# New places for the small loads at the start, and for the first and last pairs of graphs, in a two-layer graph attention kernel

## The chip, the cores and the metric

The kernel runs on one core of a Trainium2 chip. Such a core has a matrix engine (TensorE, PE in the profile), a vector engine (VectorE, DVE), an engine for functions of one argument (ScalarE, ACT), a general one (GpSimd, POOL), one that mostly issues transfers (SyncE, SP), and 16 DMA engines that move data between the main memory and the on-chip memory. Each engine works through a list of its own, in order. The metric is the time of one execution in microseconds (us); lower is better. Three executions gave a median of 2377.61 us (2377.54 to 2379.04).

## The reference

128 graphs, each of 128 nodes with 512 features, all in fp32, go through two layers. All graphs share one 128 x 128 adjacency matrix `adj`.

```python
# layer 0: attention with 8 heads of 64, masked by adj
q, k, v = (x @ Wq + bq), (x @ Wk + bk), (x @ Wv + bv)      # split into 8 heads
scores = q k^T / sqrt(64) + (1 - adj) * -1e9
out = softmax(scores) v                                     # heads joined again
x = layernorm(x + out @ Wo + bo)
# layer 1: graph attention with one head
h = x @ W
e = leaky_relu((h a1)[:, None] + (h a2)[None, :], 0.2) * adj
h' = softmax(e) h
x = layernorm(x + elu(h' + beta * h))
```

## The kernel before

**Pairs.** Two graphs are worked on at a time: 64 pairs, NG = 64, graphs 2g and 2g+1. Pair g is planned STEP = 36.678 us after pair g-1, and several pairs overlap.

**A pair's work.** The x of a pair is fetched twice: as four blocks of 512-byte rows (`load_blocks`, L81, one buffer xblk), which VectorE transposes into xT (`turn_x`, L240), and as whole graphs (`load_x`, L91), to which GpSimd adds the output bias for the residual sum (`residual`, L435). Each of the five large products (q, k, v, the output product w, and h of layer 1) is made from a two-by-two splitting of its matrices, with seven block products in place of eight: GpSimd makes sums of blocks of the input (`block_sum`, L260, tiles tx, tw, th), sums of the weights (s_q, s_k, s_v, s_w, s_h; `weight_sum`, L223 to L229) are made once at the start, TensorE makes the block products (`product`, L301 and L307, into pq, pk, pv, pw, ph and, for the products that serve both halves, eq, ev, ew, eh), and ACT (`take_part`, L349 and L355) and VectorE (`add_block`, L365) bring them together in qT, kT, v, w and h.

**Attention.** Scores (L379, psc), mask (L387), row maxima (L395), exponentials (L401) and the normalised weights (L415) follow. These go to main memory (`attn_write`, L422, tile scr) and come back in another order by four reads (`attn_read`, L427, tile ab); VectorE transposes them (`turn_attn`, L444, attnT), and TensorE multiplies by v (`attend`, L454, po). After the output product and the layer norm (L472 to L522, x1), layer 1's logits are built from two row products (L505) and brought across partitions (L536 to L556, pb, or a transfer through s2d), and its attention is applied (`aggregate`, L642, pz, evicted to zT at L649). ELU follows (L653 to L662), then the last norm (`shift` L714 on VectorE, `norm_f` L720 on ACT) and the store (L726 on SP).

**Order.** Nothing is scheduled by a planner at build time. Every step has a written place: `at(place, step, ...)` records it, all steps are sorted by place, and are emitted in that order; each engine's list is the part of it that the engine executes. `rows(g)` lists the steps of a pair with common places, `last_rows(g)` those of the last two pairs, and `other` replaces the places for pairs 0 to 3, NG-4 and NG-3. A place is a planned time, and not a wait: an instruction runs once those ahead of it on its engine are done and its inputs and buffers are there.

**The start.** x of pair 0 (four transfers), the biases and wq are issued first, from SP and ACT. GpSimd builds the identity and issues adj (L151) and, in `load_later` (place 0.583), beta, the two halves of a and the output bias bo, each broadcast to 128 rows (L104). adj is needed for the mask (`make_mask`), beta for a scaled identity (`make_beta`), a for `wa_column` (L180), which multiplies layer 1's weight by a, and bo for the residual. TensorE runs 30 matmuls on the identity (`keep_busy`, L136) and turns the biases (L140) ahead of the first product. wk and wv are issued on SP in `load_k_and_v`, wo and w1 in `load_weight`.

**The end.** The last pair's output product and h product are made in plain form (L336 and L671), for which parts of wo and w1 are loaded again into wq_sb and wk_sb (`load_again`, L124). Its graphs are normed and stored in halves (L682 to L710). The tiles u_124 to u_127 of the last two pairs are written in two buffers (tag `uf`, two buffers), so that u_126 follows u_124 in the same memory.

Of the kernel before, what the change touches and what calls it, by code (L numbers as in the profile page):

```python
# [18 lines left out]
STEP = 36.678  # L19
# [3 lines left out]
def gnn_two_layers(  # L23
# [127 lines left out]
    nc.gpsimd.dma_start(out=adj_sb, in_=adj)  # L151
    later = {}

    def load_later():
        later["beta"] = broadcast(cpool, beta, 1, "beta_b")
        for j in range(2):
            a_j = a1[j * D : (j + 1) * D].rearrange("f o -> (f o)")
            later["a", j] = broadcast(wk2, a_j, D, "uf")
        later["bo"] = broadcast(cpool, bo, D, "bo_b")
# [578 lines left out]
    def at(place, fn, *args):  # L738
        pieces.append((place, len(pieces), fn, args))
# [81 lines left out]
    def last_rows(g):  # L821

        b0, b1 = g * G, g * G + 1
        if g == NG - 2:
# [5 lines left out]
                (-20.065, product, "q", g, 6), (-18.272, product, "q", g, 7),  # L830
                (-17.379, product, "k", g, 7), (-17.337, take_part, "q", g, 6, 1, 0),
                (-16.541, fetch_x, b0), (-16.486, product, "q", g, 2), (-16.091, fetch_x, b1),
                (-15.593, product, "k", g, 1), (-14.7, product, "k", g, 2),
                (-12.947, take_part, "k", g, 1, 0, 0), (-12.481, add_block, "q", g, 2, 0, 0),
                (-12.121, add_block, "k", g, 2, 0, 0), (-10.901, residual, b0),
                (-9.651, residual, b1), (-9.477, product, "q", g, 5),
                (-8.344, take_part, "q", g, 5, 1, 1), (-7.718, product, "k", g, 6),
                (-6.585, take_part, "k", g, 6, 1, 0), (-5.093, product, "k", g, 5),
                (-3.799, take_part, "k", g, 5, 1, 1), (-3.334, product, "q", g, 3),
                (-2.499, add_block, "k", g, 7, 1, 1), (-2.441, product, "k", g, 3),  # L840
                (-2.201, take_part, "q", g, 3, 0, 1), (-2.139, add_block, "q", g, 7, 1, 1),
                (-1.548, product, "k", g, 4), (-1.308, take_part, "k", g, 3, 0, 1),
                (-0.655, product, "q", g, 4), (0.478, add_block, "q", g, 4, 1, 0),
                (1.178, add_block, "k", g, 4, 1, 0), (2.175, scores, b1), (3.322, scores, b0),
                (3.562, mask, b1, 0), (4.182, mask, b1, 1), (4.222, product, "v", g, 1),
                (4.802, mask, b0, 0), (5.285, product, "v", g, 2), (5.422, mask, b0, 1),
                (6.042, row_max, b0), (6.391, take_part, "v", g, 1, 0, 0), (7.182, row_max, b1),
                (7.382, exps, b0, 0), (7.883, product, "v", g, 6), (8.152, exps, b0, 1),
                (8.922, exps, b0, 2), (9.122, add_block, "v", g, 2, 0, 0), (9.692, exps, b0, 3),
                (10.462, exps, b1, 0), (10.481, product, "v", g, 7), (10.682, row_inv, b0),  # L850
                (11.232, exps, b1, 1), (12.002, exps, b1, 2), (12.772, exps, b1, 3),
                (13.793, row_inv, b1), (15.553, normalise, b0, 0), (16.143, normalise, b0, 1),
                (16.733, normalise, b0, 2), (17.323, normalise, b0, 3), (18.133, attn_write, b0),
                (18.917, take_part, "v", g, 6, 1, 0), (21.213, attn_read, b0),
                (21.363, normalise, b1, 0), (21.953, normalise, b1, 1), (23.073, normalise, b1, 2),
                (23.663, normalise, b1, 3), (24.473, attn_write, b1), (25.163, turn_attn, b0, 0),
                (26.143, turn_attn, b0, 1), (27.553, attn_read, b1), (32.523, product, "v", g, 5),
                (33.588, turn_attn, b1, 0), (33.629, take_part, "v", g, 5, 1, 1),
                (34.208, add_block, "v", g, 7, 1, 1), (34.568, turn_attn, b1, 1),
                (35.175, product, "v", g, 4), (36.041, product, "v", g, 3),  # L860
                (36.281, add_block, "v", g, 4, 1, 0), (37.147, take_part, "v", g, 3, 0, 1),
                (38.954, attend, b0), (40.021, attend, b1), (40.261, attend_evict, b0),
                (41.341, attend_evict, b1), (41.954, product, "w", g, 1),
                (42.641, block_sum, "w", g, 1), (42.82, product, "w", g, 2),
                (43.421, block_sum, "w", g, 2), (43.961, take_part, "w", g, 1, 0, 0),
                (44.201, block_sum, "w", g, 4), (44.401, add_block, "w", g, 2, 0, 0),
                (44.981, block_sum, "w", g, 3), (45.418, product, "w", g, 6),
                (46.284, product, "w", g, 7), (46.524, take_part, "w", g, 6, 1, 0),
# [229 lines left out]

    for g in range(NG):
        lay(g)  # L1100
    at(0.583, load_later)
    at(5.685, load_k_and_v)
    at(8.723, weight_sum, "q", 3, nc.vector)
    at(9.443, weight_sum, "q", 1, nc.vector)
# [70 lines left out]
```

## Time and profile before

| what | value |
|---|---|
| median of three executions | 2377.61 us |
| profiled execution | 2378.15 us |
| its span (first to last instruction) | 2376.4 us |
| granted TensorE clock | 0.998 |
| TensorE busy | 2354.4 us, 99% of the span |
| VectorE, ACT, GpSimd busy | 1961.7, 1591.1, 865.5 us |
| moved by DMA | 269.83 MB, 114 GB/s on average |
| wq, wk, wv landed | 10.14, 15.08, 18.15 us |
| blocks of pair 1 landed (last of four) | 23.93 us |
| scores of pair 0 begin | 28.84 us |
| from one pair's scores to the next, in the steady part | 36.50 us |

The span is what the views of the profile cover; 1.75 us of the profiled execution lie outside it. Times in the views count from the span's start. In a timeline a line gives start, duration, engine, kernel line, operation, output and inputs, count, and in brackets how long the engine stood idle before it and what ended that. SPq, POOLq and ACTq are the engines' issues of transfers. The profile names the last thing that a waiting instruction got; where that had long been done, it was another.

### The profile page before, as it was taken

Reading aid. Unit: us, or ns where it says so; the run is one execution under the profiler, and the core shown is the slowest. Engines: PE = TensorE matmul, PEld = TensorE weight load, DVE = VectorE, ACT = ScalarE, POOL = GpSimd, SP = SyncE. Lnnn points to the kernel's source line nnn. Section 1 sums busy time; section 2 is a strip of 40 time slices with the busy share of each in tenths; the row PEclk is TensorE's granted clock in tenths of the full one; section 3 lists DMA queues with packets and bytes.
Section 4 is the critical chain, followed back from the end, with each engine's and each line's share of the span. In section 5 each row is a group of like instructions: output and inputs, shape, how many; then the busy total and the mean of one; then the engine's idle time right before and its main releaser. Section 6 shows DMA issues by size and latency. Waiting matters only on the chain.

```text
span 2376.4 us, 50868 instructions
## 1 busy us (share of the span) xinstructions
PE 2354.4 (99%) x17703; PEld 2177.5 (92%) x17703; DVE 1961.7 (83%) x4390; ACT 1591.1 (67%) x5763; POOL 865.5 (36%) x1044
## 2 busy tenths in 40 slices
PE   8999999999999999999999999999999999999998
PEld 8998999999999999999999999999999999999996
DVE  7788788888888888888888888888888888888887
ACT  4675666766766667667666676676666766766665
POOL 6243333433433333334334333343343333433422
PEclk9999999999999999999999999999999999999999
DMA  6333334334343343343443433424434334344432
GB/s 192 108 100 112 116 101 125 107 105 134 92 120 119 107 118 108 108 128 92 121 122 103 119 108 111 126 92 121 123 103 119 107 112 125 92 120 122 116 115 74
DMA packets 256121, 269.83 MB, mean 114 GB/s; under 512 B 57372, under 2 KB 204840, under 8 KB 255480
## 3 DMA queue, kind: packets, MB, share of 16 engines
q1 hardware_dynamic: 254992, 265.45, 37.8%
q8 instruction: 140, 2.29, 0.4%
q14 instruction: 117, 0.96, 0.1%
q0 software_dynamic: 304, 0.85, 0.1%
q10 hardware_dynamic: 568, 0.27, 0.0%
HBM read 157.62 MB, written 108.85 MB: 112 GB/s over the span
## 4 chain that ended last, share of the span: by engine, by line
PE 96%; DMA 1%; DVE 1%; ACT 1%; issue 0%; SPq 0%; POOLq 0%; POOL 0%; DVEq 0%; ACTq 0%
PE pq L307 12%; PE pk L307 12%; PE pv L301 12%; PE ph L301 11%; PE pw L301 11%; PE eq L307 9%; PE psc L379 5%; PE po L454 5%; PE pz L642 5%; PE eh L301 5%; PE ew L301 4%; PE ev L301 4%; DMA xblk<-in_x_dram 1%; DMA wq_sb<-in_L_gnn_Wq_dram 0%; ACT s L401 0%
## 5 line engine op out<-in xcount | busy, mean ns | idle before, releaser
L435 POOL TENSOR_TENSOR x<-x,bo_b_in 128x512 f32<-128x512 f32 x128 | 163.6, 1279 | 863.3 <-DMA x<-in_x_dram 863.3
L401 ACT ACTIVATE s<-s,nmax 128x128 f32<-128x128 f32 x1024 | 396.9, 396 | 61.4 <-DVE nmax L395 61.3
L415 ACT ACTIVATE sb<-s,rinv 128x128 f32<-128x128 f32 x1024 | 325.3, 392 | 0.0
L355 ACT ACTIVATE kT<-pk,bias_c 128x128 f32<-128x128 f32 x512 | 160.2, 364 | 202.2 <-PE pk L307 143.2
L355 ACT ACTIVATE qT<-pq,bias_c 128x128 f32<-128x128 f32 x512 | 160.6, 368 | 157.6 <-PE pq L307 157.6
L505 DVE SCALAR_TENSOR_TENSOR ya<-w,wa_row 128x512 f32<-128x512 f32 x256 | 223.9, 875 | 4.4
L401 ACT ACTIVATION_READ_ACCUMULATOR s<-s,nmax 128x1 f32 x1024 | 199.2, 195 | 0.0
L466 ACT ACTIVATE oT<-po,bias_c 128x128 f32<-128x128 f32 x512 | 139.5, 382 | 80.5 <-PE po L454 80.5
L352 DVE TENSOR_TENSOR w<-pw,x 128x256 f32<-128x256 f32 x252 | 106.3, 422 | 97.3 <-PE pw L301 90.8
L444 DVE STREAM_TRANSPOSE attnT<-ab 128x512 f32<-128x512 f32 x256 | 172.7, 694 | 6.8 <-DMA ab<-scr 6.6
L387 DVE SCALAR_TENSOR_TENSOR s<-psc,amask 128x512 f32<-128x512 f32 x256 | 168.6, 680 | 0.7 <-PE psc L379 0.7
L395 DVE TENSOR_REDUCE nmax<-s 128x8 f32<-128x1024 f32 x128 | 156.1, 1220 | 4.3
L349 ACT COPY h<-ph 128x256 f32<-128x256 f32 x252 | 93.8, 372 | 94.1 <-PE ph L301 94.0
L349 ACT COPY v<-pv 128x256 f32<-128x256 f32 x256 | 94.6, 369 | 84.4 <-PE pv L301 59.9
L240 DVE STREAM_TRANSPOSE xT<-xblk 128x512 f32<-128x512 f32 x128 | 139.4, 1108 | 7.9 <-DMA xblk<-in_x_dram 7.9
L657 DVE SCALAR_TENSOR_TENSOR u<-h,x 128x512 f32<-128x512 f32 x126 | 87.1, 692 | 63.8 <-ACT h L349 61.6
L260 POOL TENSOR_TENSOR tx<-xT 128x256 f32<-128x256 f32 x128 | 94.7, 741 | 119.8 <-PE psc L379 97.1
L301 PE MATMUL pv<-wv_sb,xT 128*128 128x256 f32 x512 | 137.5, 392 | 0.0
L307 PE MATMUL pq<-xT,wq_sb 128*128 128x128 f32 x1024 | 135.9, 276 | 1.2 <-DMA wq_sb<-in_L_gnn_Wq_dram 1.2
L307 PE MATMUL pk<-xT,wk_sb 128*128 128x128 f32 x1024 | 134.8, 275 | 0.6 <-DMA wk_sb<-in_L_gnn_Wk_dram 0.4
L307 PEld LDWEIGHTS pq<-xT,wq_sb 128*128 128x128 f32 x1024 | 130.1, 193 | 4.5 <-issue 1.3
L307 PEld LDWEIGHTS pk<-xT,wk_sb 128*128 128x128 f32 x1024 | 129.1, 192 | 4.2 <-DMA wk_sb<-in_L_gnn_Wk_dram 0.6
(677 smaller groups left out, 6352.6 us busy)
## 6 DMA issues: line engine op xcount, KB each, us to landing
scr<-sb SPq DMA_DIRECT2D x128, 512.0 KB
ab<-scr SPq DMA_DIRECT2D x512, 128.0 KB
x<-in_x_dram SPq DMA_DIRECT2D x128, 256.0 KB
xblk<-in_x_dram SPq DMA_DIRECT2D x254, 128.0 KB
out_dram<-u SPq DMA_DIRECT2D x126, 256.0 KB
pb<-s2d SPq DMA_DIRECT2D x62, 128.0 KB
attd<-att SPq DMA_DIRECT2D x62, 128.0 KB
ab<-attd SPq DMA_DIRECT2D x248, 32.0 KB
```

What stands on the lines that cost most here:

```text
L301: nc.tensor.matmul(out, b[:, c, :], a[:, c, :], start=first and c == 0, stop=(c == 1), skip_group_check=True,)
L307: nc.tensor.matmul(out[:, m * N : (m + 1) * N], a[:, c, m * P : (m + 1) * P], b[:, c, :], start=first and m == 0 and c == 0, stop=(c == 1) ...
L349: nc.scalar.copy(dst, src)
L355: nc.scalar.activation(dst[:, m, :], src[:, m * N : (m + 1) * N], AF.Identity, bias=BIAS[name][:, 2 * i + m : 2 * i + m + 1],)
L387: nc.vector.scalar_tensor_tensor(s_t[b][:, j * HP : (j + 1) * HP, :], psc[b][j], SCALE, amask.rearrange("p (o n) -> p o n", o=1).broadcast ...
L395: nc.vector.tensor_reduce(nmax[b], s_t[b], AX.X, ALU.max, negate=True)
L401: nc.scalar.activation(s_t[b][:, h, :], s_t[b][:, h, :], AF.Exp, bias=nmax[b][:, h : h + 1], accum_out=rsum[b][:, h : h + 1],)
L415: nc.scalar.mul(sb[b][:, :, h, :], s_t[b][:, h, :].rearrange("p (b c) -> p b c", c=Q), rinv[b][:, h : h + 1],)
L435: nc.gpsimd.tensor_tensor(xr[b], xr[b], later["bo"], ALU.add)
L444: nc.vector.transpose(attnT[b].rearrange("p h (a r) -> p a h r", r=Q)[:, rows], ab[b].rearrange("p a (h c) -> p a h c", c=Q)[:, rows],)
L466: nc.scalar.activation(oT[b][:, c, :], src[:, c, :], AF.Identity, bias=bv_c[:, c : c + 1])
L505: nc.vector.scalar_tensor_tensor(z, y[b], 1.0, wa_row[j], ALU.mult, ALU.mult, accum_out=s12[g][:, i, j : j + 1])
```

## The change

`load_later` takes adj as well, issues bo ahead of a, and is placed at 15.913, which is behind GpSimd's four sums of x of pair 0 (places of `block_sum` "x" of pair 0 lie below it) and ahead of its sums of wv. The places of pairs 0, 1, 2, 3, NG-4, NG-3, NG-2 and NG-1, and of the steps of the start, are new; those of pairs 4 to NG-5 stay. No instruction is added or removed. On SP, x_1 now comes behind the blocks of pair 1, and wo ahead of w1. On VectorE, the sums of wk come ahead of the first add into qT, and beta's step and the products with a come later. The stores of pair 2 (last two places of its row) now come ahead of the attention reads of pair 5 (graph 10).

```diff
-    nc.gpsimd.dma_start(out=adj_sb, in_=adj)
     later = {}

     def load_later():
+        nc.gpsimd.dma_start(out=adj_sb, in_=adj)
         later["beta"] = broadcast(cpool, beta, 1, "beta_b")
+        later["bo"] = broadcast(cpool, bo, D, "bo_b")
         for j in range(2):
             a_j = a1[j * D : (j + 1) * D].rearrange("f o -> (f o)")
             later["a", j] = broadcast(wk2, a_j, D, "uf")
-        later["bo"] = broadcast(cpool, bo, D, "bo_b")
...
         2: [
...
-            102.14, 103.293, 103.497, 104.171, 105.279, 107.63, 120.701, 120.887, 122.008,
-            124.601, 125.321, 126.031, 127.821, 129.431, 130.841, 133.015, 132.265, 133.985,
-            133.235,
+            122.008, 124.601, 125.321, 126.031, 126.211, 126.561, 128.001, 129.095, 129.845,
+            130.065, 130.815,
...
-    at(0.583, load_later)
-    at(5.685, load_k_and_v)
-    at(8.723, weight_sum, "q", 3, nc.vector)
...
-    at(12.183, make_beta)
...
-    at(16.043, make_mask)
-    at(16.793, load_weight, w1_sb, w1)
...
-    at(19.493, load_weight, wo_sb, wo)
-    at(20.603, weight_sum, "v", 1, nc.gpsimd)
-    at(21.883, wa_column, 0, 0)
...
-    at((NG - 1) * STEP + -3.915, load_again, wq_sb, wo)
-    at((NG - 1) * STEP + -1.263, load_again, wk_sb, w1)
+    at(4.775, load_k_and_v)
+    at(8.593, weight_sum, "q", 3, nc.vector)
...
+    at(15.913, load_later)
+    at(16.583, load_weight, wo_sb, wo)
+    at(19.283, load_weight, w1_sb, w1)
...
+    at(27.889, make_beta)
+    at(21.5, make_mask)
+    at(30.253, wa_column, 1, 0)
...
+    at((NG - 1) * STEP + -2.156, load_again, wq_sb, wo)
+    at((NG - 1) * STEP + -0.356, load_again, wk_sb, w1)
```

The steps of pair NG-2 that end the kernel, out of its row in `last_rows` (the other rows are new in the same way):

```diff
-                (83.585, bn_stats, u, b1, "f"), (84.295, elu_sum, b0),
-                (85.015, bn_stats, u, b0, "f"), (85.725, bn_aggr, b0, "f"),
-                (85.905, bn_aggr, b1, "f"), (86.085, add_eps, g, "f"), (86.435, inv_std, g, "f"),
-                (87.555, shift, g), (87.955, norm_f, b0), (88.925, store, b0), (89.165, norm_f, b1),
-                (90.135, store, b1),
+                (84.405, bn_stats, u, b0, "f"), (85.115, bn_aggr, b0, "f"), (85.295, elu_sum, b1),
+                (86.015, bn_stats, u, b1, "f"), (86.725, bn_aggr, b1, "f"),
+                (86.905, add_eps, g, "f"), (87.255, inv_std, g, "f"), (88.375, shift, g),
+                (88.775, norm_f, b0), (89.745, store, b0), (89.905, norm_f, b1), (90.875, store, b1),
```

## The prediction

> **What bounds the kernel now.** I read the page first, for the engines' shares.
>
> ```profile
> PE 2354.4 (99%) x17703; PEld 2177.5 (92%) x17703; DVE 1961.7 (83%) x4390; ACT 1591.1 (67%) x5763; POOL 865.5 (36%) x1044
> ...
> PE 96%; DMA 1%; DVE 1%; ACT 1%; issue 0%; SPq 0%; POOLq 0%; POOL 0%; DVEq 0%; ACTq 0%
> ```
>
> TensorE is busy all the time and is 96% of the chain that ended last. The diff touches only the order near both ends, so the next view is busy time by stretch, to see where TensorE is not full (columns: stretch, length, busy us and instructions of each engine, then clock, DMA share, GB/s).
>
> ```profile
> 0.00:40.00 40.00, 34.05 (x256) 32.16 (x257) 25.09 (x46) 14.62 (x55) 21.43 (x31) 0.96 0.77 219
> ...
> 80.00:200.00 120.00, 120.00 (x911) 110.95 (x910) 97.15 (x217) 81.04 (x303) 45.55 (x55) 1.00 0.36 101
> 200.00:240.00 40.00, 37.16 (x277) 33.59 (x276) 32.20 (x75) 24.02 (x90) 13.70 (x16) 1.00 0.34 103
> ...
> 280.00:2240.00 1960.00, 1959.94 (x14838) 1821.39 (x14838) 1632.15 (x3653) 1333.40 (x4827) 711.28 (x855) 1.00 0.38 113
> ...
> 2320.00:2377.00 57.00, 44.82 (x230) 33.89 (x228) 42.41 (x118) 29.03 (x87) 12.46 (x16) 0.96 0.22 74
> ```
>
> From 280 to 2240 us TensorE lacks 0.06 us of 1960. No order can win there. All that can be won or lost lies in three places: the head (5.95 us idle), the join of pairs 2 and 3 to the steady pattern (2.84 us), and the tail (12.2 us idle). Third, the timelines of these places. The head, TensorE then VectorE:
>
> ```profile
> 25.21 1.16 PE L307 MATMUL pk<-xT,wk_sb 128*128 128x128 f32 x8 [0.28 <-DVE xT L240]
> 26.86 1.16 PE L307 MATMUL eq<-tx,wk_sb 128*128 128x128 f32 x8 [0.48 <-DVE qT L365]
> 27.85 1.06 PE L307 MATMUL pq<-xT,wq_sb 128*128 128x128 f32 x8
> ...
> 24.05 2.12 DVE L240 STREAM_TRANSPOSE xT<-xblk 128x512 f32<-128x512 f32 x2 [2.03 <-DMA xblk<-in_x_dram]
> 26.09 0.38 DVE L365 TENSOR_TENSOR kT<-eq,kT 128x256 f32<-128x256 f32 x1
> 26.39 0.41 DVE L365 TENSOR_TENSOR qT<-eq,qT 128x256 f32<-128x256 f32 x1
> ```
>
> VectorE stood still until pair 1's blocks (xblk_1) landed at 23.93; behind its two transposes stand the adds that free the buffer of eq. So xblk_1's landing already sets when TensorE gets on. The join, on SP and then VectorE:
>
> ```profile
> 203.85 1.73 SPq L427 DMA_DIRECT2D ab<-scr  x4
> ...
> 210.72 1.04 SPq L726 DMA_DIRECT2D out_dram<-u  x2
> ...
> 209.53 0.71 DVE L444 STREAM_TRANSPOSE attnT<-ab 128x512 f32<-128x512 f32 x1
> ```
>
> Graph 10's attention is read back at once, the stores of pair 2 go 7 us later, and VectorE turns the attention without a wait. The tail, ACT, VectorE and SP:
>
> ```profile
> 2362.62 0.81 ACT L720 ACTIVATE u<-u,nmr,rstdf_('f',62)_25712 128x512 f32<-128x512 f32 x1 [0.29 <-DVE nmr L714]
> ...
> 2365.56 0.76 DVE L682 SCALAR_TENSOR_TENSOR u<-plh,x 128x256 f32<-128x256 f32 x2 [2.64 <-ACT zT L649]
> ...
> 2372.05 1.80 SPq L710 DMA_DIRECT2D out_dram<-u  x4
> ```
>
> u_124 is normed at 2362.62, its store is issued at 2363.46 and lands at 2365.46; only then may L682 write u_126, which has the same buffer (tag uf, two of them). The zT named as releaser had long been done. From there to the last landing, 2375.22, is a fixed chain of 9.8 us.
>
> **What the Trainium skill says.** "DMA: Bandwidth & Descriptors", Issuing engines are not separate DMA queues: DMAs from SP, ACT and GpSimd run on the same 16 engines and interleave. The trace agrees: from 10 to 31 us the engines are full (busy share 1.06), and between 7.5 and 10.2 us packets of GpSimd's queue sat on 10 to 14 of the 16 while wq arrived. The same page, Why small descriptors are slow: fixed cost per descriptor. It agrees: blocks with 512-byte rows come at some 150 KB/us, the weights at 375 to 400. The same page, Two DMAs through the same engine are not ordered: a DMA that reads what an earlier one wrote must wait for its semaphore. So it is here: scr_10 landed at 203.83, its reads were issued at 203.85.
>
> **The change part by part.** No instruction is added or removed on any engine; 8862 matmul steps stay. Only order moves.
>
> *Head.* Five GpSimd DMAs (adj 64 KB, beta 0.5 KB, bo and twice a 256 KB each: 0.83 MB, 2.2 us of transfer at 375 KB/us) go behind pair 0's four sums of x (L260, ending at 10.53 now). The identity that TensorE's first 30 matmuls wait for comes 0.7 earlier, as adj's issue (0.71) no longer stands ahead of it on GpSimd, but bias_rows, landing at 8.71, still ends the wait before pq. Gain: wq no longer shares. It landed at 10.14; without the foreign packets I estimate 8.8, then wk 11.6 for 15.08 and wv 14.7 for 18.15. This gain does not reach TensorE's work whole. In the new order 11 product steps of 0.89 us stand behind wk's landing and end near 21.5; the next, eq from tx and wk, needs the two adds of the last fence, and these still stand behind the transposes of xblk_1. What is late next is xblk_1. It too is moved: x_1 (256 KB, 0.7 us) now goes behind it, but the 0.83 MB are now asked for at about 10.5 to 13 and share with wv, x_0 and xblk_1. If the engines move as many bytes as now up to then, it lands at 23.93 - 0.7 = 23.2; if they work at the full 385 KB/us from 5 us on (now some 270 to 10 us), up to 1.9 us earlier or a bit more, and more still if part of the late transfers comes after it: 20.5. I take 21.6. Then transposes to 23.7, adds to 24.4, eq at 24.4 instead of 26.86: -2.4. Against that, pair 1's first pk step (0.89), done ahead of eq now, is still to be done, and some 0.5 of small waits arise in the next 30 us, of the size of those at 25.21 and 26.86. Head: **-1.0**, and 1 for 1 with xblk_1: -2.1 at 20.5, +0.6 at 23.2. adj (about 15, used at 24.3), bo (19.5, used first by the residual adds, for layer norm much later), beta and a (used after 30) are hidden by up to some 8 us; w1 and wo change places, both land before their first sums.
>
> *Join.* The two stores of pair 2 now stand on SP ahead of graph 10's four reads. They wait for ACT's norm_f (L720). Pair 2's end is placed 3.2 us earlier, so with the head's shift the stores go at 210.72 - 3.2 - 1.0 = 206.5 and the reads at about 206.9 instead of 202.9 (203.85 less the shift). Issue to landing of all four took 4.56 at most, so VectorE's attnT of graph 10 can start at about 211.1; in the old order it would have started at 208.5. VectorE is held 2.6 us, and with it the qT and kT adds of pair 6 behind it (L365, at 212.41 now, 0.3 of slack): TensorE waits some 2.3 in pq_6. Behind such a wait the later ones (0.92, 0.79, 1.12 now) partly vanish: I count 0.7, 1.1 and 0.2. New sum 4.4, old 2.84 to 3.1: **+1.4**. Bounds: 0.5 if ACT is earlier, 2.5 if none of the later waits shrinks.
>
> *Tail.* From 2240 us the order of pairs 60 to 63 is new. Counting waits where a step stands right behind its producer in the new order (pq_62 behind ACT's qT, eq_62 behind the qT add, pk_62 behind kT, pv_61 behind v, pq_63, eq_63, ph_61, ph_62) and sizing them by today's like cases (0.2 to 1.1 each), I get 7.7 of idle where the old order, sized the same way, has 6.5: +1.2. Then pair 62's norm. x1_126 (L522, 0.7 to 0.9), the second emax, einv and att of pair 63 (0.28, 0.16, 0.35) now stand ahead of VectorE's last add of h_124 or of u_125, and u_125's statistics end the chain instead of running beside ACT: u_124's norm is some 2.1 later than TensorE's delay alone makes it, and the store and the 9.8 us chain follow it. Tail +3.3. Today's order also loses 1.36 us at 2334.48 (pb_62 behind s_in, VectorE held by graph 126's read back, whose write took 4.56 us); whether the new one loses it too is even: **+2.7**, from +1.2 to +4.
>
> Sum: -1.0 + 1.4 + 2.7 = +3.1. The profiled execution took 2378.15 (span 2376.4 and 1.75 around it), so it would be 2381.2; the median shown is 0.54 lower: **2380.7 us**, 0.13% slower. A measurement of this kernel can tell about 0.2%, 4.75 us, from no change; so this counts as the same.
>
> **Rivals.** (1) *Slower.* The late GpSimd transfers take xblk_1's place: they meet its 512-byte rows in the full stretch, and it lands at 24.0 or later. For: their packets held 10 to 14 engines against wq's. Against: they are done by about 17 if they move as fast as now. At 24.0 the head is +1.4, at 25 +2.4; with join and tail +5.5 to +6.5, up to +8 with the tail's upper end: 2384. It decides from a landing of 23.2 on, where the sum passes 4.75. (2) *Hidden anyway*: the moved DMAs help and hurt nothing that is waited for, and join and tail lose only half: head 0 to -1, rest +2: 2378.5. For: 99% busy. Against: the join's reads stand behind stores that wait, which no cover hides. (3) *Faster by over 0.2%*: xblk_1 at 20 (-2.6), the tail's order overlaps better than I count and wins back 3 of its 12.2 us idle: 2372. Against: pair 62's store chain stands in the way, and the head's other 2.5 + 0.7 us idle (identity, bias rows) stay.
>
> **How the numbers follow.** Likeliest 0.50 (own range 2378.5 to 2383), slower rival 0.28, hidden 0.18, faster 0.04. Of the likeliest a sixth passes +4.75. So faster 0.04, same 0.60, slower 0.36. The range leaves out the top of the slower rival and the faster one: 2376.8 to 2386.5.
>
> **What would show it.** Right: wq near 8.8, eq from tx and wk after an idle of 2 to 3 us named for qT or xT, psc of pair 0 near 26.3; SP's two stores ahead of ab's reads near 206.5, VectorE idle before attnT near 208 to 211, a wait of about 2 us in pq there; 280 to 2240 unchanged at 36.50 per pair; L720 of u_124 some 3 us later, and the last stores with it. Wrong: xblk_1 before 20 or after 24; stores issued before 204; a new wait in a pair after 8; a tail with under 10 us idle.

## The result, and the profile after

The changed kernel takes 2388.47 us (median; 2385.63 to 2389.55), against 2378.18 us for the kernel before on the same chip. The ratio is 1.0042, 95% interval 1.0032 to 1.0052: slower by 10.3 us, or 0.4%. The forecast was 2380.7 us, with a range that ended at 2386.5. The profiled execution took 2388.64 us, its span is 2386.9 us at a granted clock of 0.998, so 10.5 us more than the 2376.4 of before.

The page of the kernel after, engines' shares first and then the chain that ended last:

```profile
PE 2354.4 (99%) x17703; PEld 2177.0 (91%) x17703; DVE 1962.0 (82%) x4390; ACT 1592.1 (67%) x5763; POOL 866.7 (36%) x1044
...
PE 93%; DVE 3%; DMA 2%; ACT 1%; issue 1%; SPq 1%; POOL 0%; POOLq 0%; DVEq 0%; ACTq 0%
```

TensorE is busy for the same 2354.4 us; all that was lost is waiting. The chain says the same: TensorE's part fell from 96% to 93%, and what came in is VectorE, DMA and SP's queue. Busy time by stretch (stretch, length, busy us and instructions of TensorE, its weight loads, VectorE, ACT, GpSimd, then clock, DMA share, GB/s) tells where:

```profile
0.00:40.00 40.00, 32.08 (x246) 30.53 (x247) 22.59 (x36) 14.20 (x53) 24.22 (x34) 0.96 0.77 219
40.00:80.00 40.00, 37.91 (x295) 34.46 (x295) 34.54 (x75) 27.18 (x109) 14.99 (x15) 1.00 0.42 132
80.00:200.00 120.00, 119.30 (x928) 110.67 (x928) 96.03 (x216) 78.29 (x290) 43.71 (x53) 1.00 0.35 102
200.00:240.00 40.00, 36.03 (x272) 32.87 (x271) 29.57 (x66) 23.51 (x84) 11.65 (x15) 1.00 0.35 98
240.00:280.00 40.00, 37.67 (x280) 34.33 (x280) 31.87 (x72) 25.39 (x94) 14.62 (x18) 1.00 0.38 107
280.00:2240.00 1960.00, 1959.65 (x14791) 1820.83 (x14790) 1630.12 (x3652) 1334.87 (x4837) 713.34 (x859) 1.00 0.38 113
```

From 280 to 2240 us TensorE lacks 0.35 us, before 0.06: as foreseen, nothing happens there. The loss lies in the three places that the prediction named, and in each of them. The granted clock of the first 40 us is 0.96 in both traces, so it has no part in the difference. A second reading gives the sizes: the start of the same step on TensorE in both traces. Pair 3's scores begin 3.6 us later than before; pair 6's 7.2; the last pairs begin 7.5 late; the last store lands 10.5 late (2385.71 against 2375.22).

| place | forecast, us | measured in the trace, us |
|---|---|---|
| head | -1.0 | +3.6 |
| join | +1.4 | +3.6 |
| steady part | 0 | +0.3 |
| tail | +2.7 | +3.0 |
| sum | +3.1 | +10.5 |

**The head.** Timelines of TensorE, VectorE and GpSimd (start, us, engine, line, operation, count, idle before and what ended it):

```profile
8.20 0.20 PE L140 MATMUL early<-ident,bias_rows 12*128 12x12 f32 x1 [1.53 <-DMA bias_rows<-in_L_gnn_bv_dram]
...
13.79 1.13 PE L307 MATMUL pk<-xT,wk_sb 128*128 128x128 f32 x8 [2.04 <-DMA wk_sb<-in_L_gnn_Wk_dram]
...
26.97 1.16 PE L307 MATMUL eq<-tx,wk_sb 128*128 128x128 f32 x8 [1.47 <-DVE qT L365]
...
43.65 0.62 PE L190 MATMUL pwa<-ident,wa_col 128*128 128x128 f32 x4 [0.69 <-DVE wa_t L180]
...
51.16 1.13 PE L307 MATMUL eq<-tx,wk_sb 128*128 128x128 f32 x8 [1.21 <-DVE qT L365]
...
24.19 2.09 DVE L240 STREAM_TRANSPOSE xT<-xblk 128x512 f32<-128x512 f32 x2 [2.64 <-DMA xblk<-in_x_dram]
...
37.65 1.02 DVE L180 SCALAR_TENSOR_TENSOR wa_t<-w_sb,uf_in 128x512 f32<-128x512 f32 x1
38.71 1.64 DVE L180 SCALAR_TENSOR_TENSOR wa_t<-w_sb,uf_in 128x512 f32<-128x512 f32 x1
40.39 1.64 DVE L180 SCALAR_TENSOR_TENSOR wa_t<-w_sb,uf_in 128x512 f32<-128x512 f32 x1
42.07 0.69 DVE L180 SCALAR_TENSOR_TENSOR wa_t<-w_sb,uf_in 128x512 f32<-128x512 f32 x1
...
38.20 1.60 POOL L229 TENSOR_TENSOR s_w<-wo_sb,s_w 128x512 f32<-128x512 f32 x1
39.76 1.73 POOL L223 TENSOR_TENSOR s_h<-w_sb 128x512 f32<-128x512 f32 x1
```

And out of the kernel before, two of its eight products of w1 with a, and its one wait between the first scores and 80 us:

```profile
26.72 1.30 DVE L180 SCALAR_TENSOR_TENSOR wa_t<-w_sb,uf_in 128x512 f32<-128x512 f32 x1
...
29.42 0.87 DVE L180 SCALAR_TENSOR_TENSOR wa_t<-w_sb,uf_in 128x512 f32<-128x512 f32 x1
...
47.70 1.16 PE L307 MATMUL eq<-tx,wk_sb 128*128 128x128 f32 x8 [0.55 <-DVE kT L365]
```

Two things are to be seen. First, xblk_1 landed at 24.07, not at 21.6; the transposes, the two adds and eq follow it as the prediction had it. Second, VectorE is short of time behind the first scores. All eight products of w1 with a (`wa_column`, L180) now stand in one stretch from 36.3 to 45, where their new places put them: w1 landed at 31.5 (before at 26.4), so the first of them did not wait for it. In the kernel before three of them ran between 26.7 and 30.3, in time that VectorE had to spare. Two of the eight take 1.64 us and one 1.02 where the undisturbed ones take 0.69, while GpSimd makes its weight sums. What waits for VectorE is TensorE: pwa, eq of pair 2, and then 0.19 (pw) and 0.70 (po) more.

TensorE's waits up to 80 us add up: before 5.95 up to the first scores and 0.55 behind them; after 7.85 (ident 1.48, bias_rows 1.53, wq 1.33, wk 2.04, qT 1.47) and 2.79 (0.69 + 1.21 + 0.19 + 0.70). That is +1.9 and +2.2. The matmuls on the identity took 5.18 us in place of 5.60, which gives 0.4 back: 3.7, the 3.6 of the table. One more reading will be needed below, since it leaves the landing out: from the start of pair 0's scores to the start of pair 3's it is 88.65 us before and 92.16 after, 3.5 more. Of these about 1.2 are work that TensorE did ahead of the scores before (it is busy for 88.10 and 89.31 us in between), and the rest is waiting.

**The join.** SP, VectorE and TensorE in the kernel after; the first line is SP's write of graph 10's attention in the kernel before:

```profile
201.21 0.34 SPq L422 DMA_DIRECT2D scr<-sb  x1
...
204.96 0.34 SPq L422 DMA_DIRECT2D scr<-sb  x1
...
211.46 1.55 SPq L726 DMA_DIRECT2D out_dram<-u  x2
213.06 1.87 SPq L427 DMA_DIRECT2D ab<-scr  x4
...
218.33 0.71 DVE L444 STREAM_TRANSPOSE attnT<-ab 128x512 f32<-128x512 f32 x1 [4.22 <-DMA ab<-scr]
...
212.88 1.13 PE L301 MATMUL eh<-s_h,th 128*128 128x256 f32 x4 [0.83 <-POOL th L260]
...
220.96 1.16 PE L307 MATMUL pq<-tx,wq_sb 128*128 128x128 f32 x8 [2.52 <-DVE qT L365]
...
229.74 1.13 PE L301 MATMUL ph<-s_h,zT 128*128 128x256 f32 x4 [0.63 <-ACT h L349]
...
243.99 1.10 PE L301 MATMUL pw<-s_w,tw 128*128 128x256 f32 x4 [1.21 <-POOL tw L260]
...
247.08 1.13 PE L301 MATMUL pv<-wv_sb,tx 128*128 128x256 f32 x4 [1.12 <-ACT v L349]
```

Graph 10's attention was written at 204.96. Before, its reads were issued 2.6 us after the write (201.21 and 203.85), and VectorE turned the block without a wait. Now the two stores of pair 2 stand ahead of them, and the second is not issued before ACT has finished the second norm. The reads go 8.1 us after the write, VectorE stands 4.22 us, and TensorE 2.52 in pq. The sum of TensorE's waits here is 6.31 us, before 2.83.

**The tail.** TensorE's last products in the kernel before, and then TensorE, ACT, VectorE and SP of the kernel after:

```profile
2368.25 1.03 PE L671 MATMUL plh<-w_sb,zT 128*128 128x256 f32 x4
...
2376.46 1.03 PE L671 MATMUL plh<-w_sb,zT 128*128 128x256 f32 x4
...
2373.33 0.81 ACT L720 ACTIVATE u<-u,nmr,rstdf_('f',62)_25718 128x512 f32<-128x512 f32 x1 [0.61 <-DVE nmr L714]
...
2377.52 0.38 ACT L677 ACTIVATE h<-plh 128x256 f32<-128x256 f32 x1 [1.28 <-PE plh L671]
...
2376.26 0.76 DVE L682 SCALAR_TENSOR_TENSOR u<-plh,x 128x256 f32<-128x256 f32 x2 [2.96 <-ACT h L677]
2377.93 0.42 DVE L682 SCALAR_TENSOR_TENSOR u<-plh,x 128x256 f32<-128x256 f32 x1 [0.46 <-ACT h L677]
...
2382.53 1.80 SPq L710 DMA_DIRECT2D out_dram<-u  x4
```

TensorE's last product ends at 2377.49, before at 2369.28: 8.2 later, of which 7.5 had been brought along. From there to the last four stores it takes 5.04 us, before 2.77 (2369.28 to 2372.05). So 0.7 of the tail's loss lies ahead of the last product and 2.3 behind it, where TensorE has nothing left to do and VectorE, ACT and GpSimd work one behind the other.

### The profile page after: what moved, and what is told of

It is laid out like the page before. It is cut to its first block, busy times and chain, and to the rows that moved or that the text cites. A ratio compares the mean times of both kernels' runs of the same rounds, so it can differ in the third digit from the quotient of the medians.

```text
span 2386.9 us, 50866 instructions
## 1 busy us (share of the span) xinstructions
PE 2354.4 (99%) x17703; PEld 2177.0 (91%) x17703; DVE 1962.0 (82%) x4390; ACT 1592.1 (67%) x5763; POOL 866.7 (36%) x1044
## 4 chain that ended last, share of the span: by engine, by line
PE 93%; DVE 3%; DMA 2%; ACT 1%; issue 1%; SPq 1%; POOL 0%; POOLq 0%; DVEq 0%; ACTq 0%
PE pv L301 11%; PE pq L307 11%; PE pk L307 11%; PE ph L301 11%; PE pw L301 11%; PE eq L307 9%; PE psc L379 5%; PE po L454 5%; PE pz L642 5%; PE ev L301 4%; PE ew L301 4%; PE eh L301 4%; DMA xblk<-in_x_dram 1%; DMA ab<-scr 1%; DVE s L387 0%
```

## The experiments

The leading theory after the result was that the three places lose independently of each other. Its rival was that the head's delay alone moves the steady pattern into another phase, and that join and tail lose only because of it. The first three runs put one part of the change each into the kernel before.

**The head alone**: the late loads and the new places of the start, of pairs 0 and 1 and of the beginnings of pairs 2 and 3; the ends of pairs 2 and 3, with pair 2's stores, stay where they were. Two of its changed places:

```diff
-    at(0.583, load_later)
+    at(15.913, load_later)
...
-    at(16.793, load_weight, w1_sb, w1)
-    at(19.493, load_weight, wo_sb, wo)
+    at(16.583, load_weight, wo_sb, wo)
+    at(19.283, load_weight, w1_sb, w1)
```

> The kernel before with the change's head alone: load_later behind the sums of x, the new steps of the start, and the new places of pairs 0, 1, the beginning of 2 and of 3. Theory A (the three places lose independently, as read from the trace after: scores of pair 3 begin 3.6 us late, of pair 6 7.2 us late, the last landing 10.5 late): +3.6 us against before, about 2381.8. Theory B (the head's delay shifts the phases of transfers and engines, and join and tail lose because of it, not because of their own order): +8 to +10, with the join's extra wait for attnT in the trace.

Measured: 2380.06 us against 2377.83, ratio 1.0010 (1.0002 to 1.0018): +2.2. In the profiled execution xblk_1 landed at 17.70, 6.4 us earlier than in the kernel after with the same order, and nothing was lost up to the steady part (+0.06). The later waits were there all the same: 1.47 (pwa), 1.21 (eq), 0.19 (pw). So what was won in front of the scores, which begin 3.9 us earlier than before (24.92 and 28.84), was lost again behind them: from there to pair 3's scores it is 92.63 us against 88.65. The head's cost therefore has a part that goes with the landing, which varies from execution to execution, and a part that doesn't. This trace is of an execution on the fast side (2378.73), so its +0.06 is not the median's +2.2.

**The join alone**: the last places of pairs 2 and 3 (pair 2's are shown).

```diff
-            124.601, 125.321, 126.031, 127.821, 129.431, 130.841, 133.015, 132.265, 133.985,
-            133.235,
+            124.601, 125.321, 126.031, 126.211, 126.561, 128.001, 129.095, 129.845, 130.065, 130.815,
```

> The kernel before with the change's ends of pairs 2 and 3 alone (the stores of pair 2 ahead of graph 10's reads among them). Theory A: +3.6 us, about 2381.8; attnT of graph 10 waits some 4 us on VectorE, TensorE 2.5 us in pq of pair 6. Theory B: 0 to +1, as the head is not late.

Measured: 2381.92 us, ratio 1.0016 (1.0009 to 1.0022): +4.1; the trace shows +3.1 in the join, with 2.03 us of wait in pq. The loss arises without any delay of the head, at nearly its size.

**The tail alone**: the rows of the last four pairs and the places of `load_again`.

```diff
-                (85.015, bn_stats, u, b0, "f"), (85.725, bn_aggr, b0, "f"),
-                (85.905, bn_aggr, b1, "f"), (86.085, add_eps, g, "f"), (86.435, inv_std, g, "f"),
+                (84.405, bn_stats, u, b0, "f"), (85.115, bn_aggr, b0, "f"), (85.295, elu_sum, b1),
+                (86.015, bn_stats, u, b1, "f"), (86.725, bn_aggr, b1, "f"),
...
```

> The kernel before with the change's places of pairs 60 to 63 alone. Theory A: +3.0 us, about 2381.2, u_126 waiting some 3 us for u_124's store. Theory B: 0 to +1.

Measured: 2380.36 us, ratio 1.0009 (1.0001 to 1.0017): +2.5. The last product ends at 2367.55, the last stores go at 2372.60: 5.05 us, as in the kernel after. The three parts by their medians are 2.2 + 4.1 + 2.5 = 8.8 of 10.3 us; each is known to within 1.5 to 2 us, so the missing 1.5 can't be told from nothing. The phase rival falls: join and tail lose without the head.

**The join undone in the changed kernel**: only pair 2's two stores are put back behind the reads of graph 10, nothing else.

```diff
-            130.065, 130.815,
+            133.065, 133.815,
```

> The kernel after, with pair 2's two stores put back behind graph 10's four reads and graph 11's write on SP (places 133.065 and 133.815 for 130.065 and 130.815); no other instruction moves. If the stores that wait for ACT's last norm hold the reads, and the reads hold VectorE: attnT of graph 10 starts without a long wait, and the time falls by 2.5 to 3.6 us, to about 2385. If the other new places in the ends of pairs 2 and 3 cause the join's loss: no change, 2388.5.

Measured: 2382.51 us against 2377.83, ratio 1.0022 (1.0014 to 1.0031). The excess falls from 10.3 to 4.7. SP and VectorE of this kernel:

```profile
202.18 0.34 SPq L422 DMA_DIRECT2D scr<-sb  x1
204.82 1.73 SPq L427 DMA_DIRECT2D ab<-scr  x4
...
212.76 1.27 SPq L726 DMA_DIRECT2D out_dram<-u  x2
...
211.39 0.71 DVE L444 STREAM_TRANSPOSE attnT<-ab 128x512 f32<-128x512 f32 x1
```

The reads again go 2.6 us after the write, VectorE turns the block without a wait, TensorE's wait in pq is gone, and the four that are left (0.81, 0.63, 0.78, 1.12) are 0.5 us more than before. By the traces, then, two numbers in the written order cost 3 us in the join (waits of 6.31 and 3.34): this part of the theory is shown. The medians differ by more, 5.6 us. In the traces the rest comes from the head. It is the same in both kernels, but here xblk_1 landed at 20.93, and pair 3's scores begin 1.0 us later than before instead of 3.6.

This trace also tests the head's forecast where it should have held. 20.93 lies inside the bounds that the prediction took for the landing, and its rule gives -1.7 there. Pair 0's scores do begin 3.0 us earlier than before (25.82), near the 25.6 that the rule gives. But to pair 3's it takes 92.63 us in place of 88.65, and so the head loses 1.0 us. With such a landing too, the stretch behind the scores takes all that is won.

**What makes VectorE late in the head.** Two runs take the head alone and relieve VectorE, in different ways. In the first, w1 comes ahead of wo again and two of the eight columns go in front of the first masks:

```diff
-    at(16.583, load_weight, wo_sb, wo)
-    at(19.283, load_weight, w1_sb, w1)
+    at(19.283, load_weight, wo_sb, wo)
+    at(16.583, load_weight, w1_sb, w1)
...
-    at(32.963, wa_column, 0, 1)
+    at(23.6, wa_column, 0, 1)
-    at(35.153, wa_column, 0, 0)
+    at(22.9, wa_column, 0, 0)
```

> The kernel before with the change's head alone (as in the first of these runs), and in it layer 1's weight loaded ahead of wo again and two of the eight products with a (wa_column 0,0 and 0,1) placed ahead of the masks, where VectorE waits for the first scores; the rest of the head is unchanged. Theory C (in the new head VectorE is full from the first mask to the po products, because all products with a stand there; its last adds hold TensorE): the first po begins 1.4 to 2.7 us earlier than with the head alone for the same landing of pair 1's blocks, and the time falls to about 2378.3, against 2380.1 with the head alone. Theory D (the small waits of the new head come from TensorE's own order): no change, 2380.1.

Measured: 2378.93 us against 2377.84, ratio 1.0006 (0.9998 to 1.0015). The waits of 0.69 and 1.21 behind the scores are gone, only 0.20 (pw) is left; from pair 0's scores to pair 3's it takes 91.23 us, 1.4 less than with the head alone. In the second, GpSimd makes the sums of w1 ahead of the later sums of wo:

```diff
-    at(39.903, weight_sum, "w", 2, nc.gpsimd)
-    at(41.183, weight_sum, "w", 4, nc.gpsimd)
-    at(42.463, weight_sum, "h", 3, nc.gpsimd)
-    at(43.743, weight_sum, "h", 1, nc.gpsimd)
+    at(42.463, weight_sum, "w", 2, nc.gpsimd)
+    at(43.743, weight_sum, "w", 4, nc.gpsimd)
+    at(39.903, weight_sum, "h", 3, nc.gpsimd)
+    at(41.183, weight_sum, "h", 1, nc.gpsimd)
```

> The kernel before with the change's head alone, and in it GpSimd's sums of wo and w1 in the old order (w3, w1, h3, h1, w2, w4, h2, h4), in which h1 waits for the last product with a and holds the sums behind it. VectorE's list is unchanged. Theory E (products with a take 1.6 us for 0.69 while GpSimd sums weights, and this lengthens VectorE's full stretch): one or two of the three slow products fall to 0.69, the first po begins 1 to 2 us earlier for the same landing, and the time falls by as much, to about 2378.6. Theory D: no change, 2380.1.

Measured: 2379.36 us, ratio 1.0006 (0.9998 to 1.0014). VectorE and GpSimd:

```profile
38.96 0.69 DVE L180 SCALAR_TENSOR_TENSOR wa_t<-w_sb,uf_in 128x512 f32<-128x512 f32 x1
39.69 0.69 DVE L180 SCALAR_TENSOR_TENSOR wa_t<-w_sb,uf_in 128x512 f32<-128x512 f32 x1
...
42.63 0.69 DVE L180 SCALAR_TENSOR_TENSOR wa_t<-w_sb,uf_in 128x512 f32<-128x512 f32 x1
...
42.74 1.71 POOL L225 TENSOR_TENSOR w_sb<-w_sb 128x512 f32<-128x512 f32 x1 [6.08 <-DVE wa_t L180]
```

GpSimd's second sum of w1 overwrites what the columns read, so it waits 6.08 us for them. All eight columns take 0.68 to 0.69 us, seven of them with GpSimd idle, and pwa no longer waits (eq still waits 0.53); from pair 0's scores to pair 3's it takes 90.64 us, 2.0 less than with the head alone. So the length of 1.64 comes from GpSimd's sums beside it. The Trainium skill, "SBUF — State Buffer", Who interferes with whom, says that a VectorE instruction with two SBUF inputs contends with a GpSimd instruction that reads SBUF, and that the second to issue is held until the first is done. The traces agree. In the kernel after, the column at 38.71 began while a sum still had 1.09 us to run (38.20 to 39.80) and took 0.95 more, and so did the one at 40.39, with 1.10 left of the next sum. In the fence above, the last column began 0.11 ahead of the sum at 42.74: the column kept its 0.69, and the sum took 1.71 where undisturbed ones take 1.27.

In both runs xblk_1 landed late (22.60 and 23.23) and eq of pair 1 waited 2.19 and 3.13 us for it. These waits stand against what the reliefs won. By their times, +1.1 and +1.5, the two runs can't be told from the head alone (+2.2); the traces show what the reliefs do.

**The tail's mechanism.** The prediction put it on u_126's buffer, which u_124's store must leave first. The tail alone, with a tag of its own for the last pair's u, two buffers more:

```diff
     def end_max(b, i):
         if b not in u:
-            u[b] = wk2.tile([P, D], F32, tag="uf", name=f"u_{b}")
+            u[b] = wk2.tile([P, D], F32, tag="ue", name=f"u_{b}")
```

> The kernel before with the change's places of pairs 60 to 63 alone, and in it u_126 and u_127 in two buffers of their own (tag ue), so that they do not wait for the stores of u_124 and u_125. If the late norm of pair 62 and its store cause the tail's loss: L682 starts some 2 us earlier, the last chain is then set by TensorE's last products and ACT's exponentials, and 1.2 to 2 of the 2.5 us come back, about 2378.7. If TensorE's own waits in the new order cause it: below 0.5 us back, 2380.2.

Measured: 2380.11 us against 2377.84, ratio 1.0010 (1.0002 to 1.0018): nothing given back. VectorE of this kernel:

```profile
2364.59 0.42 DVE L682 SCALAR_TENSOR_TENSOR u<-plh,x 128x256 f32<-128x256 f32 x1
2365.86 0.42 DVE L682 SCALAR_TENSOR_TENSOR u<-plh,x 128x256 f32<-128x256 f32 x1 [0.85 <-ACT h L677]
...
2369.32 0.42 DVE L682 SCALAR_TENSOR_TENSOR u<-plh,x 128x256 f32<-128x256 f32 x1 [2.57 <-ACT h L677]
```

u_126 no longer waits for the store: its first half is written at once. But the third L682, u_127's second half, stands on VectorE ahead of u_126's remaining steps, and TensorE makes that half last. The last product ends at 2368.87, the stores go at 2373.92: 5.05 us again. The wait for the buffer had hidden an equally late one. The next run keeps the own buffer and lets TensorE and ACT make u_127's halves in the order in which VectorE takes them:

```diff
-            (52.397, end_product, b1, 0), (52.847, end_exp, b0, 1), (54.127, end_product, b1, 1),
-            (54.367, end_exp, b1, 0), (55.667, end_max, b0, 0), (56.027, end_max, b0, 1),
-            (56.097, end_exp, b1, 1), (56.387, end_sum, b0, 1), (56.807, end_max, b1, 1),
+            (52.397, end_product, b1, 1), (52.847, end_exp, b0, 1), (54.127, end_product, b1, 0),
+            (54.367, end_exp, b1, 1), (55.667, end_max, b0, 0), (56.027, end_max, b0, 1),
+            (56.097, end_exp, b1, 0), (56.387, end_sum, b0, 1), (56.807, end_max, b1, 1),
```

> The run with the change's tail alone and own buffers for u_126 and u_127, and in it graph 127's second half product made ahead of its first, with its exponential, as VectorE's list wants it (there u_127's second half comes first). If the own buffers gave nothing back because the next thing was as late (VectorE held for TensorE's very last product, in the order first half, second half): VectorE takes up u_127 1.7 us earlier, and with the store no longer waited for, 1.5 to 2.3 of the tail's 2.5 us come back: about 2378.2. If the tail's loss lies before TensorE's last product: no change, 2380.1.

Measured: 2379.15 us against 2377.55, ratio 1.0008 (1.0000 to 1.0016). Its VectorE and SP:

```profile
2368.00 0.42 DVE L682 SCALAR_TENSOR_TENSOR u<-plh,x 128x256 f32<-128x256 f32 x1 [1.19 <-ACT h L677]
...
2372.60 1.80 SPq L710 DMA_DIRECT2D out_dram<-u  x4
```

The wait is 1.19 in place of 2.57, and from the last product's end (2368.92) to the stores it is 3.68 us: 1.4 of the 2.3 come back. This is read from the traces; the times alone, +1.6 against +2.5, can't tell the two kernels apart. The other 0.9 I put down to the sum and statistics of u_126 that stand on VectorE behind that add; no run tried it.

**The loads alone**: the kernel before with only the five GpSimd loads moved and with `make_mask` and `make_beta` behind them.

```diff
-    at(0.583, load_later)
+    at(16.1, load_later)
-    at(12.183, make_beta)
+    at(27.889, make_beta)
-    at(16.043, make_mask)
+    at(16.15, make_mask)
```

> The kernel before with the small loads alone moved: adj, beta, bo and a issued by GpSimd behind its four sums of pair 0's x, mask and beta's step moved behind them; every other place is the old one, x_1 still ahead of pair 1's blocks on SP. If the loads behind wq help as the words of the change say: wq lands 1 us or more earlier and wk too, and the time falls by 0.5 to 1.5 us. If they are hidden anyway, or are paid back where they go: within 0.5 us of before.

Measured: 2379.30 us against 2377.84, ratio 1.0005 (0.9996 to 1.0013). In the profiled execution wq came 0.8 and wk 1.7 us earlier than in the trace of before, but xblk_1 at 25.71, 1.8 later, and pk of pair 1 waited 3.7 us for its transposes; the steps behind it were 3.6 us late. That is rival 1's picture. It rests on one trace, and the interval of the times takes in no change.

**The new order with the old loads**: the head alone, but the loads at the place that they had before.

```diff
-    at(15.913, load_later)
+    at(0.583, load_later)
```

> The kernel before with the change's head alone, and in it adj, beta, bo and a issued at the old place (load_later at 0.583), so that of the head only the new order of the other steps is left. If the moved loads cause the head's loss (they meet the weights and the blocks later): about 2378, the loss of 2.2 us gone. If the new order causes it (the products with a in VectorE's full stretch, weights of layer 1 behind wo): 2380 as with the head alone or more, wq landing 1 us later, waits of about 1 us each for wa_t and for qT left in the trace.

Measured: 2381.70 us against 2378.30, ratio 1.0016 (1.0010 to 1.0023). With late loads the same order cost 2.2, with early ones 3.4; the two intervals overlap. TensorE of this kernel:

```profile
11.35 3.48 PE L307 MATMUL pq<-xT,wq_sb 128*128 128x128 f32 x16 [0.47 <-DMA wq_sb<-in_L_gnn_Wq_dram]
...
43.22 0.62 PE L190 MATMUL pwa<-ident,wa_col 128*128 128x128 f32 x4 [0.53 <-DVE wa_t L180]
...
50.74 1.13 PE L307 MATMUL eq<-tx,wk_sb 128*128 128x128 f32 x8 [1.22 <-DVE qT L365]
```

The first product starts at 11.35, 1.6 us later than in the kernel after (9.73) and 2.7 later than with the head alone (8.65), and the waits behind the scores are there again (0.53, 1.22). So with the new order the moved loads don't make the head slower, if anything they help; what is slow is the order. The same with both reliefs of VectorE, the columns and the sums as above:

```diff
-    at(15.913, load_later)
+    at(0.583, load_later)
...
+    at(16.583, load_weight, w1_sb, w1)
...
+    at(23.6, wa_column, 0, 1)
...
+    at(39.903, weight_sum, "h", 3, nc.gpsimd)
```

> The same with layer 1's weight ahead of wo, two products with a ahead of the masks and GpSimd's weight sums in the old order: the new head with early loads and a relieved VectorE. If both terms found are all that the head loses: 2376 to 2378, no slower than before, and the waits for wa_t and qT after the first scores gone. If not: 2379 or more.

Measured: 2380.03 us against 2378.30, ratio 1.0008 (1.0001 to 1.0014). The reliefs are worth 1.7 us, clear of the noise of 21 executions each, and near the 1.3 us of waits that they remove in the traces (pwa's 0.53 gone, eq from 1.22 to 0.47). What is left, 1.7, stands in front of the scores: xblk_1 was turned at 26.07 in this trace, and eq of pair 1 waited 2.48.

**Can the landing be mended?** Two runs tried to take the late loads off xblk_1's path. In the first, with the head alone, the loads go behind GpSimd's first sum of wv:

```diff
-    at(15.913, load_later)
+    at(20.0, load_later)
```

> The kernel before with the change's head alone, and in it the small loads one place later on GpSimd: behind its first sum of wv, which waits for wv (load_later at 20.0 for 15.913). Theory F (the moved loads, adj's 512-byte rows first, meet wv and x_0 between 12 and 18 us when these are not through, and this is what makes the landing of pair 1's blocks vary from 17.7 to 24.1 with the new head): wv lands near 14 to 15 and pair 1's blocks before 20.5, the runs spread less than the 4.4 us of the head alone, and the median falls by 1 to 2 us, to about 2378.5. Theory G (the landing varies with the memory's speed in the first 10 us, whatever stands behind): the landing stays spread, 2380.1.

Measured: 2379.00 us against 2377.55, ratio 1.0007 (0.9998 to 1.0015). xblk_1 landed at 17.5 and nothing was lost ahead of the scores (pair 0's po even begins 0.56 earlier than before). But this is the trace of the fastest of its 13 executions, and they spread as widely as those of the head alone, 4.2 us against 4.4. Placing the loads later still did not take the spread away; whether they make it, this run can't say. The second has both reliefs too, and x_0 behind xblk_1:

```diff
-            15.112, 16.005, 16.658, 11.883, 17.791, 20.23, 16.898, 20.143, 19.337, 27.753, 20.47,
+            15.112, 16.005, 16.658, 12.7, 17.791, 20.23, 16.898, 20.143, 19.337, 27.753, 20.47,
...
-    at(15.913, load_later)
+    at(20.0, load_later)
```

> The head alone with all that was found put together: the small loads behind GpSimd's first sum of wv, pair 1's blocks ahead of x_0 on SP, layer 1's weight ahead of wo, two products with a ahead of the masks, GpSimd's weight sums in the old order; join and tail as in the kernel before. If pair 1's landing and VectorE's full stretch were the head's two terms: pair 1's blocks land before 20, no wait for eq above 0.6 after the scores, first po 2 to 3 us earlier than in the kernel before, 2375 to 2376. If something else holds the head: 2378 or more.

Measured: 2379.64 us against 2377.55, ratio 1.0008 (1.0000 to 1.0016). Here wv landed at 17.7 and xblk_1 at 21.6, although the loads were not even issued before 19.0. So the weights themselves came slower in this execution, and not because of these loads. In return, what comes late is now waited for. VectorE, and then TensorE:

```profile
25.88 0.69 DVE L165 TENSOR_SCALAR amask<-adj_sb 128x128 f32<-128x128 f32 x1 [1.38 <-DMA adj_sb<-in_adj_dram]
...
28.15 1.06 DVE L180 SCALAR_TENSOR_TENSOR wa_t<-w_sb,uf_in 128x512 f32<-128x512 f32 x1 [1.24 <-DMA uf_in<-in_L_gnn_a_dram]
...
37.17 2.05 PE L301 MATMUL pv<-s_v,tx 128*128 128x256 f32 x4 [3.10 <-DVE v L365]
```

The mask waited for adj, a column for a, and the masks, maxima and the add into v that stand behind them on VectorE came late; TensorE waited 3.10 us for that add.

No version was faster than the kernel before. The best by its median was the head with earlier columns, 1.1 us above it, with an interval that takes in no change.

## Why the prediction was wrong

**What held.** The three places, the empty steady part, the chain xblk_1, transposes, adds, eq, and the stores ahead of the reads. The prediction's head came from a landing at 21.6 and its rule of 1 for 1. With the measured 24.07 that rule gives eq at 26.9 (measured 26.97) and the scores at 28.8 (28.92).

**Head, two terms.** First, the landing: "I take 21.6" out of bounds of 20.5 and 23.2; it was 24.07, outside them, and beyond the point from which rival 1 was to decide. This is 2.5 of the miss in this trace. The 21.6 was not a bad middle, as the five traces with this order up to xblk_1 have 24.07, 17.70, 20.93, 22.60 and 23.23, 21.7 in the mean; what failed is bounds of 2.7 us for something that varies by 6.4. Rival 1 had it that the late loads take xblk_1's place; the trace with the loads alone fits that; but in the last run above the weights came slowly before those loads were issued, so their share can't be told from the rest, and how much of the 2.5 is theirs stays open. The record has one more hint. A transfer's semaphore rises in 16 steps, and in the trace of the kernel after 14 of the 16 of xblk_1's last block were there by 20.00, the last at 24.07; of wv's, 14 by 13.73 and the last two at 18.3 and 18.4; and two of wq's 16 were already 1.0 us behind the others before the late loads were issued. So in this trace the landing is late because two parts of 16 lag, and not because the whole is slow; why they do, no run shows.

Second, "some 0.5 of small waits arise in the next 30 us" was sized by the waits at 25.21 and 26.86 and not by what VectorE has to do there. It was 2.2 more than the 0.55 of before, so 1.7 of the miss. This is the step that failed whatever the landing: the prediction counted 0.89 and 0.5, 1.4 in all, for what comes behind the scores, and from pair 0's scores to pair 3's it was 3.5 more than before in the kernel after and 4.0 more in two others with this head, which landed early (92.63 against 88.65 in both). The diff showed the columns moved behind the masks; the work of VectorE from the first mask to po, added up beside the time for it, would have shown that it doesn't fit. Both reliefs confirm this term by their traces, and the pair of runs with early loads by its times too. Of the 4.6 us between -1.0 and +3.6 the two terms are 4.2.

**Join.** Here 2.2 us were missed, in the term "Behind such a wait the later ones (0.92, 0.79, 1.12 now) partly vanish: I count 0.7, 1.1 and 0.2". The wait itself came out at its size, 2.3 forecast and 2.52 measured, but in part by luck. The second store, 1.5 us behind the first, holds the reads until 1.6 us later than forecast once the head's delay is taken off (213.06 - 3.6 = 209.5; forecast 206.9 with a head at -1.0, so 207.9), and from their issue to VectorE's start it was 5.27 us for the 4.2 counted. So VectorE stood 4.22 us for the 2.6 forecast. That TensorE's wait came out near its forecast all the same is because 1.7 us of this stayed hidden from it, for the 0.3 counted. But the waits behind it (0.63, 1.21, 1.12) come to 2.96 us for the 2.0 counted, and one of 0.83 ahead of it is new. The profile names ACT and GpSimd for them. With the stores put back the four fall only from 3.8 to 3.3 us, so most of this belongs to the new order of the ends of pairs 2 and 3 and not to the stores; which of the moved steps makes it, no run shows. The bound of 2.5, "if none of the later waits shrinks", was passed too. (The parts of the forecast, 2.3, 0.7, 1.1 and 0.2, make 4.3 and not 4.4.)

**Tail.** Right in size, +3.0 for +2.7, and right that most of it comes behind the last product: 2.3 there for 2.1. Ahead of it the size is in part luck. The forecast was 1.2 more of waits less half of the 1.36 for s_in. That wait (1.20) went away wholly, and TensorE lost 0.7 all the same, so the other waits grew by some 1.9. Behind the last product two things hold the chain, and only one was seen. The store of u_124 does hold u_126, but without it the order of u_127's halves holds VectorE just as long. Both mended give 1.4 us back, the buffer alone nothing; the halves alone were not tried.

**The case that came.** It was rival 1's side, slower, at 10.3 us where its worst sum was 8. All three places came out worse than forecast, the head by 4.6, the join by 2.2 and the tail by 0.3, and the range, which left out the top of this rival, had no room for that.

## What to carry to other kernels

When an order is changed at a kernel's head, add up each engine's work in the stretches it is moved into, and against the idle time it is moved out of; a wait that is not in the old trace can't be sized by the small waits that are. A transfer placed ahead of others on an in-order queue costs not its own time but that of the engine it waits for, to everything behind it: here reads that went 2.6 us after their write went 8.1 us after it. And when a wait is removed and nothing changes, look for the second one that ended just as late.

## What was not expected of the hardware

The landing of the same transfer, in the same order, varies by 6 us between executions: xblk_1 at 24.07 in the kernel after, 17.70 with the head alone, 20.93 with the stores put back. Between wk's and wv's landing, 1 MB, lay 2.5 to 4.8 us. The times spread accordingly. The standard deviation of the executions is 0.7 to 1.4 us in the kernel before and in every run that keeps its head's order (the loads alone among them, 1.3), and 1.0 and 0.9 with the new head and early loads. In the six runs that have the new head and late loads it is 1.4 to 2.5, some 2.0 together. So the scatter goes with the late loads in the new order; how they make it, no run shows. A single trace of such a head shows one case of many.

A VectorE product of 128x512 takes 0.69 us with GpSimd idle and 1.64 when it begins with over 1 us of a GpSimd sum still to run, and the sums between such products go from 1.27 to between 1.60 and 1.84 us. In the kernel after, that adds about 2.2 us to the VectorE stretch that TensorE waits for (0.95 + 0.95 + 0.33).
